# Gate logits from the values' normalised tokens instead of a second normalisation

## The chip, the cores and the metric

One core of one Trainium2 chip runs the kernel. The metric is the device time of one execution in microseconds; a lower time is better.

## The reference

The input is `x` of shape (4, 56, 56, 128): four images of 3136 tokens with 128 channels. Four layers follow one another: a neighbourhood attention with a feed-forward part, a recurrence over a spectrum, a softmax attention with a mixture of eight experts (two per token), and the layer that this change touches. The last layer is, for the tokens `t` of one image:

```
t = t + L3_attn(ln(t))        # q, k, v from ln(t); attention = softmax(exp(-|q-k|^2)) @ v
x = ln(t)                     # normalised over the 128 channels, no weight, no bias
logits = x @ gate_w.T + gate_b                  # 64 experts
probs  = softmax(logits, over the tokens)
vals, idx = top_k(probs of each expert, 8)      # eight tokens for every expert of every image
pooled = sum over the 8 of vals * x[idx]        # one vector per expert and image
out    = second product of a gelu feed-forward of the expert on pooled
result = t + scatter_add(out * vals at idx)
```

In the attention of this layer, `exp(-|q-k|^2)` is practically zero for every pair of tokens, so the softmax is uniform and the attention adds one and the same vector `v = Wv mean(ln(t))` to all tokens of an image. The kernel uses that, and verifies on the chip with bounds on the distances that it holds.

## The kernel before

**Sizes.** An image's tokens lie in `NT` = 28 tiles of `P` = 112 tokens; `GT` = 4 tiles make a group, so an image has `NG` = 7 groups of `GW` = 448 tokens. A tensor with tokens on the partitions is 112 x 512 per group; turned, it is 128 x 448. There are `EC` = 64 experts and `KT` = 8 tokens for each.

**Two layernorms.** For the last layer the kernel normalises each token twice: once before the mean of the values is known (`g_st`, `g_rs`, `g_off` in `span_norms`, `xn` in `normal`, line L1693) and once after `v` has been added (`c_st`, `c_rs`, `c_off` in the choice's `statistics` and `root`, `xn` again by `normal`). `FarAttention.of` makes the first: four `xn` per group on ACT, four transposes on PE (`turned`, L208 is the helper that records every transpose), a copy `xnT` that also sums over the tokens (L1813), the products q and k with bfloat16 casts (`products`) and their norms (`with_norms`). `FarAttention.mean` makes `v` from the sums (`x_total`, `v_ps` L1883, `v` L1887) and `add` adds it to the tokens (`x` L1892 on DVE). `bounds` are the bfloat16 products `d_ps` (L1861), each followed by an ACT relu with a sum (L1873) or a DVE reduction (L1867); one piece of it is called a half.

**The expert choice** is `ExpertChoice.steps`. For each group: `statistics` (four DVE instructions, L2301), then `root` (a Newton iteration on DVE, `inverse_root`, L909 ff.), `store` (two DMAs on SP: the tokens, then `c_rs` as a column of single numbers, into the DRAM table `rows` that the later gather reads), and then by group `tokens` (`normal`: four ACT instructions, for image 3 every second on POOL, L1688), `turned` (four PE transposes, one ACT copy `zT` L2322), and `logits` (PE product `l_ps` L2327, ACT copy `taken` L2331, DVE MAX8 `best` L2332, which takes from the PSUM). After all groups, `choose` finds the positions of the eight largest (FIND_INDEX8, L2351) and POOL gathers the rows (L2355), `marked` marks them (L2363), `weighed` multiplies (L2377), and `pooled` reduces.

**Where the work lies.** `Attention.run` is layer 2's softmax attention, one image after another, made of score products `s_ps` (L2066) and output products `o_ps` (L2149). Between these, `Paced` calls pieces of a background list as their due times come. A piece has a cost, which fixes its due time in its list, and can be marked `apart`, so that no second of its list begins in the same step. Behind image 2's attention stand the mixtures and far pieces of images 0 and 1 and the choice of image 0 (`chosen(0)`, merged with the bounds); behind image 3's stand the mixture and far pieces of image 2 and the choices of images 1 and 2. `trail(3)` lets the groups of image 3 follow its own attention block by block (places "t").

The order that results is written out and rearranged by a scheduler for each engine; each engine then runs its queue in order. After the attention, a part with an order written out by hand follows (`tc.manual_schedule`, L3006): the last group's far pieces, `mean`, `add` and `statistics`, `root` for groups 0 to 2 and for groups 3 to 6, then `tokens`, `turned` and `logits` of the seven groups of image 3 interleaved by hand with halves (`beside`), the choice, and after it `experts`, which streams 32 weight lots of 1 MB, and `scatter`. Nine lots are requested before the mean.

Of the kernel before, what the change touches and what calls it, by code (L numbers as in the profile page):

```python
# [1699 lines left out]
class FarAttention:  # L1700
# [16 lines left out]
    def __init__(self, env, ctx, flow, work):  # L1717
        self.env, self.flow, self.work = env, flow, work
# [31 lines left out]
    def weights(self):  # L1750
# [25 lines left out]
        def of_values():  # L1776
            ps = flow.one([128, 512], "w_ps")
            nc.tensor.transpose(ps[:, :C], loaded("w_v", ins["L3_attn_Wv"]), env.ident)
            self.v_w = cp.tile([128, C], F32, tag="v_w", name="v_w")
            nc.vector.tensor_copy(self.v_w, ps[:, :C])  # L1780
# [13 lines left out]
    def image(self, b, spans, places="d"):  # L1794
# [4 lines left out]
        x = env.x[b]  # L1799
        held = {"q": {}}  # L1800
        pool = self.held[1 - b % 2]

# [75 lines left out]
        def mean():  # L1878
            total = sp.tile([128, 1], F32, tag="x_total", name="x_total")
            nc.vector.tensor_reduce(total, held["sums"], AX.X, ALU.add)  # L1880
            nc.vector.tensor_scalar(total, total, 1.0 / TOK, None, ALU.mult)
            v_ps = flow.one([128, 512], "v_ps")
            nc.tensor.matmul(  # L1883
                v_ps[:P, :C], total.to_broadcast([128, P]), self.v_w, start=True, stop=True
            )
            held["v"] = v = sp.tile([P, C], F32, tag="v", name="v", bufs=1)
            nc.vector.tensor_copy(v, v_ps[:P, :C])  # L1887

# [8 lines left out]
        def of(span):  # L1897
            take, norm = span_norms(env, sp, b, span, places)

            def tokens(g):  # L1900
                held["xn"] = normal(
                    env, self.work, places, b, g, norm, span, places == "t" and g == NG - 1
                )

            return [costing(1.8 * len(span), take)] + sum([
                [
                    costing(0.6, lambda g=g: tokens(g)), costing(0.6, lambda g=g: turned(g), True),
                    costing(0.8, lambda g=g: products(g), True),
# [308 lines left out]

class ExpertChoice:
# [9 lines left out]
    def __init__(self, env, ctx, flow):  # L2228
# [24 lines left out]
        ]  # L2253
        self.fold = cp.tile([2 * EC, EC], F32, tag="fold", name="fold")
        nc.gpsimd.tensor_tensor(self.fold, env.ident[:, :EC], env.ident[:, EC:], ALU.add)
        self.lots, self.at = {}, 0

# [7 lines left out]
    def pieces(self, b, places="d"):  # L2265
# [5 lines left out]
        for g in range(NG):  # L2271
# [10 lines left out]
    def steps(self, b, places, norms_of):  # L2282
# [20 lines left out]
        def root(groups):  # L2303
            of = slice(groups[0] * GT, (groups[-1] + 1) * GT)
            mean2, var = moments(env, sp, f"c{len(groups)}", st[:, of, :])
            inverse_root(env, sp, var, rs[:, of])
# [26 lines left out]

        def store(groups):
            of = slice(groups[0] * GT, (groups[-1] + 1) * GT)
            rows_of = self.rows[b].rearrange("(t p) c -> p t c", p=P)
# [54 lines left out]
        def pooled():  # L2391
# [13 lines left out]
            logits=logits, choose=choose, marked=marked, weighed=weighed, gather=gather,  # L2405
# [100 lines left out]
    def scatter(self):  # L2506

        env, nc, flow = self.env, self.env.nc, self.flow
        for pair in range(2):
# [4 lines left out]
            bias = self.late.tile([2 * EC, C], F32, tag="c_bias", name="c_bias")  # L2514
# [382 lines left out]
def layers_of_safe_scores(env: Env, f, soft):  # L2897
    with ExitStack() as ctx:
# [63 lines left out]
        def chosen(b):  # L2962
            return listed("far", held["choice"].pieces(b))

        def to_mixture():
# [3 lines left out]
            held["far"] = far = FarAttention(env, right, flow, held["choice"].work)  # L2969
# [36 lines left out]
        with tc.manual_schedule(  # L3006
# [5 lines left out]
            *tail, products, with_norms = held["tails"][-1]  # L3012
# [17 lines left out]
            for g in early:  # L3030
                add[g]()
                of["statistics"](g)
                beside("scalar", 1)
            of["root"](early)
            of["store"](early)
            each("statistics", late)
            beside("scalar", 1)
            of["tokens"](0), of["tokens"](1), of["turned"](0), of["logits"](0)
            of["root"](late)
            of["store"](late)  # L3040
            of["turned"](1), of["tokens"](2), of["logits"](1), of["turned"](2), of["logits"](2)
            beside("scalar", 1)
            of["tokens"](3), of["tokens"](4), of["turned"](3)
            of["tokens"](5), of["logits"](3), of["turned"](4)
            of["tokens"](6), of["logits"](4), of["turned"](5), of["logits"](5)
            of["turned"](6), of["logits"](6)
# [90 lines left out]
```

## Time and profile before

| | |
|---|---|
| median of 3 runs | 2461.78 us |
| lowest and highest | 2459.37 and 2465.88 us |
| the profiled execution | 2462.98 us, of which its span is 2461.2 us |
| granted TensorE clock, mean of the span | 0.965 |
| busy share of PE, DVE, ACT, POOL | 95%, 74%, 63%, 12% |
| last layer-2 attention to the first expert product | 2275 to 2342 us |
| expert products and scatter to the end | 2342 to 2461 us |
| DMA in the last slices of the span | up to 297 GB/s |

Times inside the span are counted from its start. The engines are named PE (matmul), PEld (weight load), DVE, ACT, POOL and SP (the queue that issues most DMAs). A row of groups names the line, the engine, the operation, the output and input, their shapes, the count, then the busy time in us, the mean duration in ns, and the idle time just before with what ended it.

### The profile page before, as it was taken

To read this page: it belongs to the slowest core of one execution; us is meant where nothing else is said; L and a number is where in the kernel's file an instruction comes from. 1 tells how busy PE (TensorE), PEld (TensorE's weight loads), DVE (VectorE), ACT (ScalarE), POOL (GpSimd) and SP (SyncE) were. 2 spreads that over 40 slices of the span, in tenths; PEclk is the share of its full clock that TensorE was granted. 3 is DMA by queue.
4 is the path that set the end of the run, shared out by engine and by line. 5 is a ranking of instruction groups with operands and counts; after the bars stand their busy time and mean duration, and the time that the engine had idled before them with its cause. 6 is when DMAs were issued, how large, how long until landed. Compare 5 with 4: busy or idle time off the path is not lost.

```text
span 2461.2 us, 38767 instructions
## 1 busy us (share of the span) xinstructions
PE 2337.9 (95%) x14357; PEld 1258.2 (51%) x14357; DVE 1816.2 (74%) x4816; ACT 1550.7 (63%) x3346; POOL 293.8 (12%) x578
## 2 busy tenths in 40 slices
PE   6999999999999999999999999999999998998585
PEld 4777777775455555555554444445444443433134
DVE  5666899983997958799678777854788576776554
ACT  4999889875666646676332556575545566775553
POOL 4423363320000000000000000100000001011302
PEclk9999999999999999999999999999999997998578
DMA  5100000000000000000000010000000010100676
GB/s 124 36 8 2 2 2 2 2 2 9 1 1 1 1 1 0 1 1 1 12 1 0 1 27 1 5 1 1 1 1 1 1 27 5 27 5 1 184 297 206
DMA packets 65642, 61.42 MB, mean 25 GB/s; under 512 B 17048, under 2 KB 60915, under 8 KB 61348
## 3 DMA queue, kind: packets, MB, share of 16 engines
q1 hardware_dynamic: 64932, 57.80, 8.4%
q8 instruction: 115, 1.88, 0.3%
q0 software_dynamic: 512, 1.06, 0.2%
q14 instruction: 83, 0.68, 0.1%
HBM read 45.83 MB, written 12.90 MB: 24 GB/s over the span
## 4 chain that ended last, share of the span: by engine, by line
PE 63%; DVE 6%; ACT 2%; DMA 2%; issue 2%; POOL 1%; SPq 0%; DVEq 0%; POOLq 0%; ACTq 0%
PE s_ps L2066 20%; PE o_ps L2149 20%; PE y_ps L1574 7%; PE d_ps L1861 3%; PE xT_ps L208 2%; PE g_ps L1207 2%; DMA lot<-in_L_ffn_lots 2%; PE l_ps L2327 1%; PE y_ps L2090 1%; PE z_ps L2042 1%; PE q_ps L1825 1%; DVE found L1867 1%; PE l_ps L1534 1%; ACT xn L1693 1%; DVE gated L1587 1%
## 5 line engine op out<-in xcount | busy, mean ns | idle before, releaser
L2073 ACT ACTIVATE e<-s_ps 128x448 f32<-128x448 f32 x688 | 366.5, 541 | 491.8 <-PE s_ps L2066 486.1
L2066 PE MATMUL s_ps<-zT,xnT 128*128 128x448 f32 (+1 forms) x1400 | 649.4, 554 | 0.0
L2149 PE MATMUL o_ps<-e,keep 128*128 128x448 f32 (+1 forms) x1376 | 648.5, 554 | 0.0
L2149 PEld LDWEIGHTS o_ps<-e,keep 128*128 128x128 f32 (+1 forms) x1376 | 241.7, 190 | 217.8 <-issue 217.2
L2066 PEld LDWEIGHTS s_ps<-zT,xnT 128*128 128x128 f32 (+1 forms) x1400 | 241.1, 189 | 213.9 <-issue 193.5
L1873 ACT ACTIVATE d_ps<-d_ps,half 128x448 f32<-128x448 f32 (+1 forms) x376 | 227.2, 605 | 88.0 <-PE d_ps L1861 86.3
L1867 DVE TENSOR_REDUCE found<-d_ps 128x1 f32<-128x448 f32 x324 | 196.9, 619 | 77.6 <-PE d_ps L1861 75.7
L1574 PE MATMUL y_ps<-experts,xnT 128*112 128x512 f32 x448 | 217.0, 608 | 0.0
L1587 DVE TENSOR_TENSOR gated<-y_ps,gate 112x512 f32<-112x512 f32 x220 | 148.8, 686 | 35.5 <-PE y_ps L1574 33.0
L1593 DVE TENSOR_TENSOR gated<-gated 112x512 f32<-112x512 f32 x330 | 151.8, 467 | 3.5
L1861 PE MATMUL d_ps<-q_near,k_near 32*128 32x448 bf16 (+1 forms) x700 | 135.4, 374 | 15.6 <-ACT d_ps L1873 10.0
L208 PE MATMUL xT_ps<-ident,xn 112*128 112x112 f32 x672 | 117.8, 283 | 34.1 <-ACT xn L1693 26.0
L208 PEld LDWEIGHTS xT_ps<-ident,xn 112*128 112x128 f32 x672 | 80.4, 147 | 113.5 <-ACT xn L1693 58.9
L1673 POOL TENSOR_TENSOR g_rs<-var,exponent 112x4 f32<-112x4 f32 x17 | 17.9, 1053 | 1006.3 <-DVE var L1672 895.3
L1574 PEld LDWEIGHTS y_ps<-experts,xnT 128*112 128x112 f32 x448 | 77.2, 180 | 98.9 <-issue 63.8
L1861 PEld LDWEIGHTS <-k_near 32*128 32x128 bf16 (+1 forms) x700 | 32.0, 92 | 181.2 <-issue 167.2
L1693 ACT ACTIVATE xn<-x,g_off,g_rs 112x128 f32<-112x128 f32 x220 | 93.2, 486 | 26.3 <-DVE g_off L1675 13.0
L677 DVE TENSOR_TENSOR e<-e,band 112x1792 f32<-112x1792 f32 (+3 forms) x56 | 99.9, 1788 | 10.2 <-ACT e L670 10.2
L782 PE MATMUL f_ps<-w_fc,h 128*112 128x128 f32 x896 | 104.8, 274 | 1.9 <-ACT h L773 1.6
L782 PEld LDWEIGHTS f_ps<-w_fc,h 128*112 128x112 f32 x896 | 99.8, 177 | 5.2 <-ACT h L773 4.8
L768 PE MATMUL h_ps<-zT,w_fc 128*128 128x448 f32 x224 | 88.9, 540 | 0.6 <-ACT zT L762 0.6
L670 ACT ACTIVATE e<-s_ps 112x1792 f32<-112x1792 f32 (+3 forms) x56 | 82.6, 1476 | 6.3 <-PE s_ps L661 3.3
(427 smaller groups left out, 3939.7 us busy)
## 6 DMA issues: line engine op xcount, KB each, us to landing
lot<-in_L_ffn_lots SPq DMA_DIRECT2D x32, 1024.0 KB
out_x<-x SPq DMA_DIRECT2D x28, 224.0 KB
x<-in_x SPq DMA_DIRECT2D x3, 1568.0 KB
rows<-x SPq DMA_DIRECT2D x3, 1568.0 KB
x<-in_x SPq DMA_DIRECT2D x7, 224.0 KB
parts<-in_waves SPq DMA_DIRECT2D x8, 173.0 KB
out<-found SPq DMA_DIRECT2D x60, 2.0 KB
rows<-x SPq DMA_DIRECT2D x1, 896.0 KB
```

The lines of the kernel that those rows point to most:

```text
L208: self.nc.tensor.transpose(ps[:, j * P : (j + 1) * P], xn[:, j, :], self.ident[:P, :P])
L782: nc.tensor.matmul(f_ps[:, j, :], h[:, k, j * P : (j + 1) * P], w_fc2[:, k, :], start=(k == 0), stop=(k == 3),)
L1574: nc.tensor.matmul(y_ps, held["xnT"][g][:, j * P : (j + 1) * P], self.experts[:, 4 * i : 4 * i + 4, :], start=True, stop=True,)
L1587: nc.vector.tensor_tensor(gated[:, some, :], y_ps, gate[:, some].unsqueeze(2).to_broadcast([P, 4, C]), ALU.mult,)
L1593: by.tensor_tensor(gated[:, :n, :], gated[:, :n, :], gated[:, n : 2 * n, :], ALU.add)
L1693: env.nc.scalar.activation(xn[:, j, :], env.x[b][:, g * GT + j, :], AF.Identity, bias=norm["off"][:, i : i + 1], scale=norm["rs"][:, i : i ...
L1861: nc.tensor.matmul(d, held["k"][part, 128 * c : 128 * c + n], held["q"][g][part, :], start=True, stop=True,)
L1867: nc.vector.tensor_reduce(self.found[:, self.most : self.most + 1], d, AX.X, ALU.max)
L1873: nc.scalar.activation(d, d, AF.Relu, bias=self.half[:n], accum_out=self.found[:n, self.sums : self.sums + 1],)
L2066: nc.tensor.matmul(s_ps[i * n : (i + 1) * n, :GW], self.xnT[:, at : at + n], zT, start=True, stop=True,)
L2073: nc.scalar.activation(e[:n], s_ps[:n, :GW], AF.Exp)
L2149: nc.tensor.matmul(sums[:, :GW], self.keep[:n, k, :], e[:n], start=(k == 0 and g - 1 not in pairs), stop=last,)
```

## The change

The second layernorm and its turn are not done any more. With `d = 1/g_rs`, `w` the gate weights with their mean over the channels taken off, and `m = w v` (one number per expert), the logits of a token are

```
logits = c_rs * (d * (w xn) + m)
```

where `xn` is the token normalised before `v` was added. `w xn` is made in the far pieces from `xnT`, right after it was turned for q and k. The product of Wv with `w` is made once in the setup and `m` from it with one small matmul per image.

The per-token scales `d` and `c_rs` lie with tokens on the partitions, but the logits have experts on the partitions and tokens in the row. For images 0 to 2, `keep_scales` stores both into DRAM and `fetch_scale` fetches them group by group, broadcast over 64 partitions; POOL multiplies by `d`, and DVE adds `m` and multiplies by `c_rs` in one instruction, then takes the maximum from the SBUF (`moved`). For image 3, `d` of the first six groups is fetched and multiplied in the far pieces; `d` of the last group and all of `c_rs` are spread with PE products of a broadcast column and the identity (`spread`), and the DVE instruction reads the result from the PSUM. `root` for image 3 uses a POOL power in place of the Newton iteration. The part written out by hand is shorter: seven `moved`, each followed by one half.

```
 FarAttention.weights / of_values
+            self.choice.centre()
-            nc.vector.tensor_copy(self.v_w, ps[:, :C])
+            nc.tensor.matmul(
+                ps[:, C : C + EC], w_v, self.choice.gate_w, start=True, stop=True
+            )
+            nc.vector.tensor_copy(self.v_w, ps[:, : C + EC])
 FarAttention.image / mean
+            m_ps = flow.one([128, 512], "m_ps")
+            nc.tensor.matmul(m_ps[rows, :1], self.v_w[:, C:], total, start=True, stop=True)
+            nc.scalar.copy(choice.moved[b // 2][rows], m_ps[rows, :1])
 FarAttention.image / of
+            def deviations():
+                held["sd"] = sd = sp.tile([P, n], F32, tag=f"g_sd{n}_{places}", name="g_sd", bufs=1)
+                nc.vector.reciprocal(sd, norm["rs"])
+                if not final:
+                    choice.keep_scales(b, 0, span, sd)
+                    return
+                ps = flow.one([128, 512], "sd_ps")
+                choice.spread(ps, rows, sd)
+                held["row"] = row = sp.tile([128, GW], F32, tag="row_t", name="row", bufs=1)
+                nc.scalar.copy(row[rows], ps[rows, :GW])
             def tokens(g):
...
+                if trailing and not final:
+                    held["row"] = row = sp.tile([128, GW], F32, tag="row_t", name="row", bufs=1)
+                    choice.fetch_scale(row[rows], b, 0, g)
+            def logits(g):
+                cols = slice(g * GW, (g + 1) * GW)
+                l_ps = flow.one([128, 512], "l_ps")[rows, :GW]
+                nc.tensor.matmul(l_ps, choice.gate_w, held["xnT"], start=True, stop=True)
+                if final:
+                    nc.vector.tensor_tensor(raw[:, cols], l_ps, held["row"][rows], ALU.mult)
+                    return
+                nc.scalar.copy(raw[:, cols], l_ps)
+                if trailing:
+                    nc.gpsimd.tensor_tensor(
+                        by_tile(raw[:, cols]), by_tile(raw[:, cols]),
+                        by_partition(held["row"][rows]), ALU.mult,
+                    )
 ExpertChoice
+    def keep_scales(self, b, i, span, scale):
+        of = slice(span[0], span[-1] + 1)
+        self.env.nc.sync.dma_start(
+            self.scales[b][i].rearrange("g (p j) -> p g j", p=P)[:, of],
+            scale.rearrange("p (g j) -> p g j", j=GT),
+        )
+    def fetch_scale(self, row, b, i, g):
+        self.env.nc.sync.dma_start(row, self.scales[b][i][g].partition_broadcast(EC))
+    def spread(self, ps, rows, scale):
+        for j in range(GT):
+            self.env.nc.tensor.matmul(
+                ps[rows, j * P : (j + 1) * P], scale[:, j : j + 1].to_broadcast([P, EC]),
+                self.env.ident[:P, :P], start=True, stop=True,
+            )
 ExpertChoice.pieces, for images 0 to 2 (from_raw=True): in place of tokens, turned, logits
+            for cost, name in ((0.1, "fetched"), (1.4, "moved")):
+                first.append(costing(cost, lambda name=name, g=g: steps[name](g)))
 ExpertChoice.steps
         def root(groups):
-            inverse_root(env, sp, var, rs[:, of])
+            if last:
+                nc.vector.tensor_scalar(var, var, 1e-5, None, ALU.add)
+                nc.gpsimd.tensor_tensor(
+                    rs[:, of], var, env.exponent[:P, : var.shape[1]], ALU.pow
+                )
+            else:
+                inverse_root(env, sp, var, rs[:, of])
+        def fetched(g):
+            held["scale"] = scale = [
+                self.work.tile([128, n], F32, tag=f"{tag}_d", name="scale", bufs=1)[rows, :GW]
+                for tag, n in (("xn", GT * C), ("xnT", GW))
+            ]
+            for i in range(2):
+                self.fetch_scale(scale[i], b, i, g)
+        def moved(g):
+            part = taken[:, cols]
+            if last:
+                ps = flow.one([128, 512], "rs_ps")
+                self.spread(ps, rows, rs[:, g * GT : (g + 1) * GT])
+                scale = ps[rows, :GW]
+                nc.vector.scalar_tensor_tensor(
+                    part, part, self.moved[b // 2][rows], scale, ALU.add, ALU.mult
+                )
+            else:
+                apart, scale = held["scale"]
+                nc.gpsimd.tensor_tensor(
+                    by_tile(part), by_tile(part), by_partition(apart), ALU.mult
+                )
+                nc.vector.scalar_tensor_tensor(
+                    by_tile(part), by_tile(part), self.moved[b // 2][rows],
+                    by_partition(scale), ALU.add, ALU.mult,
+                )
+            nc.vector.max(held["best"][rows, g * KT : (g + 1) * KT], part)
         def store(groups):
+            if not last:
+                self.keep_scales(b, 1, groups, rs[:, of])
 the part written out by hand, image 3
+            logits()
             of["root"](early)
             of["store"](early)
             each("statistics", late)
-            beside("scalar", 1)
-            of["tokens"](0), of["tokens"](1), of["turned"](0), of["logits"](0)
+            beside("scalar", 2)
             of["root"](late)
             of["store"](late)
-            of["turned"](1), of["tokens"](2), of["logits"](1), of["turned"](2), of["logits"](2)
-            beside("scalar", 1)
-            of["tokens"](3), of["tokens"](4), of["turned"](3)
-            of["tokens"](5), of["logits"](3), of["turned"](4)
-            of["tokens"](6), of["logits"](4), of["turned"](5), of["logits"](5)
-            of["turned"](6), of["logits"](6)
+            for g in range(NG):
+                of["moved"](g)
+                beside("scalar", 1)
             of["choose"]()
```

## The prediction

> **What bounds the kernel now.** The page came first, its engine line and its slices. Digits are tenths of a slice of 61.5 us; PEclk is the granted TensorE clock.
>
> ```profile
> PE 2337.9 (95%) x14357; PEld 1258.2 (51%) x14357; DVE 1816.2 (74%) x4816; ACT 1550.7 (63%) x3346; POOL 293.8 (12%) x578
> ...
> PE   6999999999999999999999999999999998998585
> ...
> PEclk9999999999999999999999999999999997998578
> DMA  5100000000000000000000010000000010100676
> ```
>
> TensorE is busy at 9 tenths from slice 1 on (counted from 0) except in slice 33, where busy share and clock dip, and in the last slices; only there is room. In the attention phase (1380 to 2275 us) only what leaves or enters PE's queue moves the end; work taken off ACT, DVE or POOL there is worth nothing by itself.
>
> Next, the table by windows. Columns: stretch, length, busy us (instructions) of PE, weight load, DVE, ACT, POOL, granted clock, DMA share, GB/s.
>
> ```profile
> 2020.00:2040.00 20.00, 19.66 (x79) 8.21 (x77) 7.87 (x18) 17.14 (x45) 0.00 (x0) 1.00 0.08 1
> 2040.00:2060.00 20.00, 15.62 (x47) 6.31 (x47) 9.98 (x33) 13.66 (x35) 1.01 (x1) 0.65 0.00 1
> 2060.00:2080.00 20.00, 18.55 (x42) 6.23 (x41) 13.90 (x27) 13.19 (x28) 6.21 (x10) 0.75 0.06 14
> 2280.00:2300.00 20.00, 8.52 (x24) 3.09 (x24) 13.45 (x56) 9.55 (x27) 10.85 (x13) 0.50 1.00 408
> 2300.00:2320.00 20.00, 14.57 (x33) 5.08 (x34) 6.03 (x22) 10.72 (x25) 3.49 (x8) 0.50 0.92 146
> 2320.00:2340.00 20.00, 9.71 (x30) 1.85 (x28) 14.58 (x25) 12.34 (x29) 5.09 (x11) 0.50 0.06 13
> ```
>
> Two places fall short: 2040 to 2080 (image 1's choice, clock 0.65 and 0.75) and the tail (image 3's choice, PE half idle at clock 0.50). The waits of PE name the first, and PE's groups from 2045.5 to 2065.6 show what it cost:
>
> ```profile
> PE xT_ps L208 <- ACT xn L1693: 2.7, 1, 2.7
> ```
> ```profile
> L2327 PE MATMUL l_ps<-zT,gate_w 128*64 128x448 f32 x6 | 4.9, 911 | 1.0 <-ACT zT L2322 1.0
> L208 PE MATMUL xT_ps<-ident,xn 112*128 112x112 f32 x12 | 4.3, 428 | 2.7 <-ACT xn L1693 2.7
> ```
>
> In that stretch the list had put choice transposes, gate matmuls and bound products one after another with no attention matmul between; PE waited 2.7 us for ACT's normalised tokens, and the clock's events show 0.5 from 2046.0 to 2069.9. A transpose took 428 ns, not 259, a gate matmul's instruction 911, not 564.
>
> Last, the chain of waits through the tail (start, length, what):
>
> ```profile
> 2294.74 1.65 ACT xn L1693 x4
> 2296.39 0.49 ACT zT L2322
> 2296.88 0.04 issue
> 2296.93 1.75 PE l_ps L2327 x2
> 2298.68 0.95 PE xT_ps L208 x4
> 2299.65 0.54 ACT zT L2322
> ...
> 2321.27 0.54 ACT taken L2331
> 2321.83 0.65 DVE best L2332
> ```
>
> Seven groups go through one loop, copy 0.54, gate product 1.75, transposes 0.95: 3.3 us each, 2294.7 to 2322.5. From there the pick runs serially to the first expert product at 2342.
>
> **The sum** is made against the profiled execution, 2462.98 us (span 2461.2 and 1.78 around it), 1.20 above the median of 2461.78.
>
> *A. PE work in the attention phase.* Images 0 to 2 lose 21 groups of four transposes. At full clock four take 0.47 us of PE time (pitch of 228 instructions from 1384 to 2040: 26.8 us). Two lie wholly in the slow stretch, so 19 x 0.5 = -9.5. Their 21 gate matmuls only move into the far pieces, each with its ACT copy (0.526). Image 3's first six groups bring theirs from the tail: 6 x 0.9 (pitch per matmul, two instructions) = +5.4. Centring the gate and the extra product with Wv: +1. A = -3. ACT loses 84 normalisations (0.488) and 21 copies (0.531) here, DVE gains 21 fused products (0.615, the row of L2377): off PE's path, counted at nothing. PE's own queue covers them; without that cover DVE's is +13.
>
> *B. The slow stretch.* From the gate product at 2045.5 to the next attention product at 2065.6 there are 20.0 us holding 7.8 us of work at full pitch; with the half-speed tail to 2069.9 it lost about 14.5. In the changed order of PE's queue no run without attention matmuls is estimated over 5 us (the longest before: 14.7), and the chain xn, transposes, copy, gate product is gone. I take -12; bounds 0 (a like stretch forms elsewhere) and -17.
>
> *C. Setup and copies of the mean* (four m_ps products beside v_ps, 0.335 each by that row, ACT copies): inside A's rounding.
>
> *D. The tail.* Added ahead: the last group's reciprocal on DVE, four PE spread matmuls and an ACT row copy stand in front of its normalisation: 0.2 + 1.75 (as one gate product at half clock) + 0.5 = +2.4. The second Newton root (12 steps of about 0.2) becomes one POOL power (1.05, row L1673), as does the first: about -1.2 each. Then seven `moved` steps with no round trip between them: on DVE one fused product from PSUM (0.68, row L1849) and one MAX8 (0.65), 1.35 each, 9.5 in all; on PE four 112-column matmuls that together stream as many columns as one gate product (1.75 at half clock) and a bound half (about 0.5): 2.3 each, 16 in all. The early statistics ended at 2290.35; with 2.4, a root of 1.9 (0.5 of small steps, the power, 0.35), four late groups' statistics (0.88 each) and the second root of 1.9 the first `moved` starts near 2300, and the last maximum falls between 2310 and 2317 by which engine limits; I take 2313.5 against 2322.5: D = -9, bounds -12 and -5. The rows' store, landed by 2316.6, still ends before the gather needs it; a last maximum before 2312 would make it late next.
>
> *E. New waits.* Before each choice `c_rs` is stored (SP, behind nothing, but ahead of 1.6 MB of rows), then each group fetches two broadcast rows on SP; POOL multiplies, DVE fuses. Nearest rows: a 64 KB load landed in 1.5 us, the 12.5 KB of 4-byte elements (`rows<-c_rs`) in 4.9 alone; so root to first fetch is some 6 us, against 4 to 7 us of other DVE work queued between: up to 2 us of DVE wait per image, and up to 1 us per group where the list leaves under 2 us between `moved` steps. SP gets 58 DMAs more in all (10 stores, 48 fetches of 64x448); its own queue holds little else then: the lots of 1 MB are issued only after the last far piece, so nothing waits behind these but the rows' stores and, for the trailing groups of image 3, one fetch and one POOL product each. Both scale buffers are single, so a fetch waits for the step before. One fetch of image 1 stands on SP behind a 10.6 us rows store; POOL's multiply waits for it, and behind POOL's queue the next power `g_rs`, which ACT's normalisation and PE's transposes need. POOL gains 27 products of about 1.1 us (L2539's 1274 ns x 448/512). The floor is 0, attention work hiding all (a gain is excluded: nothing here is removed); the ceiling is 21 x 1 = 21. PE has other matmuls queued through most of it, so I take near the floor, +4.
>
> The port shared by DVE and POOL speaks against E's floor: in the tail a DVE step on 12 columns (L938) took 1.12 us beside a POOL add, 0.17 elsewhere. The Trainium skill, SBUF — State Buffer, "SBUF: two separate sides", says that a DVE instruction with two SBUF inputs and a GpSimd instruction reading SBUF lock each other out for the whole instruction; by it alone every one of the 27 products could block one DVE step, which DVE's 26% of idle time absorbs or not as E's bounds say.
>
> A + B + D + E = -3 - 12 - 9 + 4 = -20: 2443 profiled, **2442** on the median's scale.
>
> On the clock the row says that 2.7 us of idle was enough for 24 us at half speed. The Trainium skill, TensorE: Matmul & The Clock Gate, "HAM oscillation", blames idle gaps over about 3.4 us; by it a fetch wait of 2 us costs its own length alone, by the row several times that.
>
> **Rivals.**
>
> *The slow stretch stays (15%).* Far pieces still hold xn, transposes and copies in series, and one PE wait of over 2 us is enough. Then B = 0: 2454. Against it: the changed queue spreads them between attention matmuls.
>
> *Slower: fetches stall POOL and through `g_rs` PE (17%).* Place: the seven `moved` steps of images 0 to 2. Price: if a PE idle of over 2.5 us follows in each image, three stretches like the present one, 3 x 14.5 = 43, replace E's 4: 2482; with two, 2467. Decides where the fetch lands over 3 us after the DVE's queue reaches `moved`. For it: single buffers, in-order SP, 4.9 us small-element stores. Against: PE's queue holds attention work throughout, and only the mixture pieces behind `g_rs` would run late.
>
> *The tail is bound by PE at half clock (inside my forecast).* 16 us from 2301: last maximum 2317, D = -5, time 2446.
>
> *It doesn't do what it says (3%).* The unscaled logits need their own normalisation only if transposes remain; the queue shows 112 fewer, so little speaks for it.
>
> **How the numbers follow.** My forecast 65%, spread 2432 to 2450 by the terms' bounds. The low end of the range is A at its best (0.6 per four transposes, 0.75 per gate product: -7) with B -17, D -12 and E +2: -34, so 2428 on the median's scale; 2427 taken. The high end takes in the stretch that stays and part of the slow rival, 2466. A tenth lies above, less below. What a measurement of this kernel can tell from no change is about 0.3%, 7.4 us: faster means under 2454.4, slower over 2469.2. Forecast and two fifths of the first rival are faster: 0.65 + 0.06 = 0.71; the rest of that rival (0.09), the part of the slow rival in which two images stall (0.03) and the change without effect (0.03) are the same: 0.15; the slow rival's rest, 0.14, is slower.
>
> **What would show it.** Right: L208 down by 112 transposes, no window of 20 us between 1400 and 2270 under clock 0.9, first fetch landing before DVE is ready, last MAX8 of the tail about 33 us after the last `g_rs` (2280.33 before) rather than 42. Wrong: PE waits on POOL or DVE `moved`, DVE idle released by DMA of the scales, half-clock stretches about 1520, 2050 or 2150, or a tail loop over 2.5 us per group.

## The result, and the profile after

The change made the kernel slower: 2484.4 us median (2482.4 to 2486.1) beside 2461.5 us of the kernel before, a ratio of 1.0090 with an interval of 1.0073 to 1.0108. The profiled execution took 2483.9 us, its span 2482.1. The forecast was 2442. The experiments ran on several chips, on which the median of the kernel before was 2458.1 to 2461.7 us; so from here on every ratio is against the kernel before on the same chip, and differences in us between versions are worked out from their ratios.

The page of the changed kernel, engine line and slices (62.1 us each):

```profile
PE 2335.6 (94%) x14321; PEld 1255.3 (51%) x14321; DVE 1842.6 (74%) x4827; ACT 1511.2 (61%) x3238; POOL 327.9 (13%) x593
...
PE   6999999999999999999999999999999999998575
...
PEclk9999999999999999999999999999999999998588
DMA  5100000000000000000000011000000011200576
```

At this grain almost nothing is seen: ACT lost 40 us of work, POOL gained 34, the dip of the clock in slice 33 is no longer a digit. The windows show it (columns as before):

```profile
2020.00:2040.00 20.00, 14.79 (x44) 5.31 (x43) 12.56 (x37) 8.20 (x21) 6.43 (x5) 0.95 0.51 97
2040.00:2060.00 20.00, 17.61 (x65) 7.11 (x65) 16.73 (x57) 13.83 (x36) 8.21 (x7) 0.88 0.16 37
2060.00:2080.00 20.00, 12.73 (x39) 5.87 (x37) 9.37 (x19) 7.04 (x19) 5.34 (x6) 0.74 0.27 41
2300.00:2320.00 20.00, 8.59 (x28) 3.52 (x28) 8.75 (x32) 8.66 (x26) 11.99 (x12) 0.52 0.85 341
2320.00:2340.00 20.00, 14.49 (x61) 9.24 (x62) 11.95 (x35) 7.88 (x23) 3.38 (x2) 0.50 0.85 214
```

From 2020 to 2080 PE works 45.1 of 60 us (before: 53.8 in the same stretch), and ACT and DVE have no more to do than PE. So the engines stand still together, and not for lack of queued work. The waits of PE (2030 to 2080) and of DVE (2000 to 2080) name what they wait for:

```profile
PE xT_ps L208 <- ACT xn L1693: 13.3, 2, 7.3
```
```profile
DVE g_off L1675 <- POOL g_rs L1673: 8.7, 2, 7.5
DVE taken L2451 <- DMA scale<-scale: 4.0, 1, 4.0
```

The timelines of SP, POOL, DVE, ACT and PE give the first of the two stalls link by link (start, length, engine and line, and in brackets the idle time before with what ended it):

```profile
2026.03 0.58 SPq L2462 DMA_DIRECT2D rows<-x  x1
2029.83 9.61 SPq L2333 DMA_DIRECT2D scale<-scale  x2
```
```profile
2037.62 1.35 POOL L2448 TENSOR_TENSOR taken<-taken,scale 64x448 f32<-64x448 f32 x1 [7.81 <-DMA scale<-scale]
2039.05 1.01 POOL L1673 TENSOR_TENSOR g_rs<-var,exponent 112x4 f32<-112x4 f32 x1
```
```profile
2031.89 0.14 DVE L1672 TENSOR_SCALAR var<-var 112x4 f32<-112x4 f32 x1
2031.95 0.61 DVE L1875 TENSOR_REDUCE found<-d_ps 128x1 f32<-128x448 f32 x1
2040.09 0.16 DVE L1675 SCALAR_TENSOR_TENSOR g_off<-sums,g_rs 112x4 f32<-112x4 f32 x1 [7.53 <-POOL g_rs L1673]
```
```profile
2040.29 1.65 ACT L1693 ACTIVATE xn<-x,g_off,g_rs 112x128 f32<-112x128 f32 x4 [7.17 <-DVE g_off L1675]
```
```profile
2040.83 0.83 PE L208 MATMUL xT_ps<-ident,xn 112*128 112x112 f32 x2 [6.04 <-ACT xn L1693]
```

In order of time: SP issues the store of 1.6 MB of rows, then the fetch of a scale, which lands 7.8 us later instead of the usual 2.67. POOL's product with 1/g_rs waits for that. The variance of image 3's next group is ready on DVE at 2032.0, but its power stands behind the product in POOL's queue and starts at 2039.05. DVE's next instruction, `g_off`, needs the power, so DVE stands still for 7.5 us with everything behind it, then ACT for 7.2, then PE for 6.0. The late fetch of one row of scales stops four engines.

The second stall (7.3 us of PE idle up to 2073.3) is the same with DVE in POOL's place: its fused product waits 4.0 us for a row of `c_rs` that was only just stored, and the variance that POOL's power needs stands behind it. The chain of waits shows it, and POOL's timeline two products that ran beside it:

```profile
2060.63 6.26 DMA scale<-scale
2066.91 1.84 DVE taken L2451
...
2069.83 0.18 DVE var L1672
2070.14 1.02 POOL g_rs L1673
2071.18 1.31 DVE g_off L1675
```
```profile
2066.60 1.34 POOL L2448 TENSOR_TENSOR taken<-taken,scale 64x448 f32<-64x448 f32 x1 [6.58 <-DMA scale<-scale]
2071.12 1.34 POOL L2448 TENSOR_TENSOR taken<-taken,scale 64x448 f32<-64x448 f32 x1
```

Two DVE instructions are longer here than elsewhere, the fused product (1.84 us, median 1.02) and `g_off` (1.31 us, 0.16 in the first stall), both beside a POOL product; together that is some 2 of the 7.3 us.

In the tail the chain of waits of the changed kernel shows one step of the seven, and their end:

```profile
2330.24 1.72 PE rs_ps L2338 x8
2331.97 0.50 PE d_ps L1869
2332.47 0.02 issue
2332.49 0.73 ACT d_ps L1881 x2
...
2342.34 0.64 DVE best L2455
```

The last steps take 3.06 us each and are serial: spread 1.72 to 1.77, bound products 0.5, ACT's sum 0.73. From the start of the last `g_rs` to the last maximum it is now 39.5 us (2303.5 to 2343.0), before 42.2.

The loss of this profile, 20.9 us of span, lies in the attention phase (the last output product of layer 2 starts at 2265.1, before at 2246.6: +18.5) and between that and the last `g_rs` (+4.6: the transposes, the gate, q, k and norm products of the group before the last all come behind the last output product now; before, its transposes came ahead); the tail gives 2.7 back. The kernel's description and the prediction count the attention phase to 2275 us; that takes in the mixture of the last group.

### The profile page after: what moved, and what is told of

Read it like the earlier page. It is cut to its first block, busy times and chain, and to the rows that moved or that the text cites. A ratio compares the mean times of both kernels' runs of the same rounds, so it can differ in the third digit from the quotient of the medians.

```text
span 2482.1 us, 38731 instructions
## 1 busy us (share of the span) xinstructions
PE 2335.6 (94%) x14321; PEld 1255.3 (51%) x14321; DVE 1842.6 (74%) x4827; ACT 1511.2 (61%) x3238; POOL 327.9 (13%) x593
## 4 chain that ended last, share of the span: by engine, by line
PE 58%; DVE 9%; DMA 4%; ACT 2%; POOL 2%; issue 1%; SPq 0%; DVEq 0%; POOLq 0%; ACTq 0%
PE s_ps L2106 18%; PE o_ps L2189 18%; PE y_ps L1574 7%; PE d_ps L1869 3%; PE g_ps L1207 2%; PE xT_ps L208 2%; DMA scale<-scale 2%; DMA lot<-in_L_ffn_lots 2%; DVE found L1875 1%; PE l_ps L1933 1%; PE q_ps L1833 1%; DVE gated L1587 1%; PE y_ps L2130 1%; PE z_ps L2082 1%; PE l_ps L1534 1%
## 5 line engine op out<-in xcount | busy, mean ns | idle before, releaser
L1869 PE MATMUL d_ps<-q_near,k_near 32*128 32x448 bf16 (+1 forms) x700 | 137.3, 376 | 21.6 <-ACT d_ps L1881 10.2
L1673 POOL TENSOR_TENSOR g_rs<-var,exponent 112x4 f32<-112x4 f32 x17 | 18.1, 1062 | 894.6 <-DVE var L1672 894.5
L208 PE MATMUL xT_ps<-ident,xn 112*128 112x112 f32 x560 | 94.2, 277 | 27.3 <-ACT xn L1693 18.9
L208 PEld LDWEIGHTS xT_ps<-ident,xn 112*128 112x128 f32 x560 | 64.8, 144 | 82.9 <-ACT xn L1693 43.4
```

Of the source, the lines that this page charges most:

```text
L208: self.nc.tensor.transpose(ps[:, j * P : (j + 1) * P], xn[:, j, :], self.ident[:P, :P])
L1869: nc.tensor.matmul(d, held["k"][part, 128 * c : 128 * c + n], held["q"][g][part, :], start=True, stop=True,)
```

## The experiments

A table of the attention phase, worked out from PE's records from 1200 us to the last output product: gaps and durations are summed, and the time at half clock is from the clock's events. Each row is the one profiled execution, in us.

| kernel | last output product | PE idle | PE busy | at half clock |
|---|---|---|---|---|
| before | 2246.6 | 12.4 | 1033.5 | 30.2 |
| the change | 2265.1 | 32.9 | 1032.0 | 34.1 |
| scales resident, 8 byte step | 2232.7 | 7.6 | 1024.9 | 10.2 |
| scales resident, 16 byte step | 2241.2 | 11.2 | 1029.4 | 13.3 |
| product with 1/g_rs early | 2248.9 | 19.3 | 1029.6 | 23.9 |
| the same, c_rs resident | 2235.9 | 11.5 | 1024.2 | 6.8 |

The last column is not wholly due to waits: in the change, 6.8 of its 34.1 us (from 1788.7) follow a stretch in which no gap of PE is over 0.05 us.

**Which images.** First, images 0 to 2 as before (`from_raw=False`, no `deviations` and no `logits` in their far pieces, no `keep_scales`), image 3 as changed:

```
-            return listed("far", held["choice"].pieces(b, from_raw=True))
+            return listed("far", held["choice"].pieces(b))
...
-                    costing(0.6, lambda g=g: logits(g), True),
+                    *([costing(0.6, lambda g=g: logits(g), True)] if trailing else []),
```

> Only image 3 takes its logits from the values' tokens; images 0 to 2 normalise and turn a second time as before. Theory (the fetches of the scales in images 0 to 2 cost the time, the tail gains the 2.6 us that the two profiles show): the attention phase goes back to its old length plus six gate products (about 5 us), so 2459 to 2467 us. Rival (the loss lies in image 3's steps, or in the reordered queue as a whole): 2475 us or more.

Measured: ratio 1.0048 (1.0032 to 1.0063), 2469.1 us. The theory gave at most 2467 and the rival at least 2475, so this is between the two. In the profile PE's time to the last output product grew by some 11 us of work and 2.8 of idle; six gate products are 5.4 of that by the prediction's price, and time at half clock rose to 37.5 us; the tail gave back 2.7. So image 3's part alone is a loss as well. That its gate products moved out of the tail, where PE has room, into the attention phase, where it has none, explains about half of the 11 us; the rest is not followed further.

Then the reverse, images 0 to 2 as changed, image 3's far pieces, `root` and hand-written order as before:

```
-            trailing, n = places == "t", len(span) * GT
+            trailing, n = False, len(span) * GT
...
-            for g in range(NG):
-                of["moved"](g)
-                beside("scalar", 1)
+            of["tokens"](0), of["tokens"](1), of["turned"](0), of["logits"](0)
+            ...
```

> Images 0 to 2 as in the change, image 3 as before. Theory: the loss stays, less the six gate products that stay in the tail, plus the 2.6 us of the tail: 2477 to 2488 us. Rival (image 3's steps): within 6 us of 2461 us.

Measured: 1.0095 (1.0071 to 1.0119), 2479.7 us, PE idle 31.3. The first three images' part alone loses as much as the whole change. The two parts do not add up (0.48% and 0.95% against 0.90% together); that each moves the other's pieces is the likely reason, not a shown one.

**Waits or work.** Both scales read from a resident tensor of other numbers, the instructions left as they are:

```
-            for i in range(2):
-                self.fetch_scale(scale[i], b, i, g)
+            held["scale"] = [
+                self.bias1.rearrange("q c e -> q (c e)")[rows, : 2 * P]
+                .rearrange("q (p j) -> q j p", p=P)[:, :1, :].to_broadcast([EC, GT, P])
+            ] * 2
...
```

> In images 0 to 2 both scales are read from a resident tensor of other numbers, so no fetch is made and the selection differs; all engine instructions stay (the resident rows are read with a step of 8 bytes, the fetched ones of 16). Theory (waits for the fetches): most of the loss goes, 2445 to 2462 us. Rival (load and port contention of POOL's 21 products and DVE's 21 fused products, or the order of the queues): 2475 us or more.

Measured: 0.9917 (0.9898 to 0.9936), 2438.6 us: by the ratios some 43 us less than the change, and, at 2441 us on the scale of the first chip, where the forecast was. The same windows of this kernel:

```profile
2020.00:2040.00 20.00, 19.71 (x71) 7.35 (x70) 16.98 (x57) 15.49 (x41) 2.35 (x2) 1.00 0.24 35
2040.00:2060.00 20.00, 18.86 (x69) 8.75 (x67) 18.45 (x54) 11.39 (x30) 2.46 (x4) 1.00 0.13 2
2060.00:2080.00 20.00, 19.82 (x57) 6.84 (x56) 18.73 (x47) 14.21 (x32) 5.88 (x10) 1.00 0.06 14
```

PE is full at full clock. All 21 POOL products and 21 fused DVE products are still made, so neither their number nor their place beside one another is the main cost. (The fetched rows also lay in buffers that the far pieces use; in the trace of the change no engine but SP waits for these to come free.) But this kernel changed two things: the resident row has a step of 8 bytes between its numbers, the fetched rows one of 16. So it was run again with 16 (`p=P // 2`, and the same with eight parts of 56):

> As the kernel with resident scales, but these are read with the step of 16 bytes that the fetched rows have, so that the fused DVE instruction and the POOL product last as long as in the change (1.07 and 1.42 us in place of 0.67 and 1.18); no fetch, other numbers. Theory (waits): within 4 us of the kernel with the 8 byte step. Rival (length of the strided instructions carries part of the gain): 2448 us or more.

Measured: 0.9953 (0.9936 to 0.9970), 2450.3 us, which is the rival's number and not within the theory's 4 us; the two intervals touch only at 0.9936. The rows of the fused DVE product, in this order of the kernel with an 8 byte step, with 16, and (from the version with the first groups on PE, below) read from the PSUM without a step:

```profile
L2449 DVE SCALAR_TENSOR_TENSOR taken<-taken,moved,bias 64x448 f32<-64x448 f32 x21 | 14.1, 674 | 0.2
```
```profile
L2448 DVE SCALAR_TENSOR_TENSOR taken<-taken,moved,bias 64x448 f32<-64x448 f32 x21 | 21.3, 1018 | 0.2
```
```profile
L2448 DVE SCALAR_TENSOR_TENSOR taken<-taken,moved,rs_ps 64x448 f32<-64x448 f32 x9 | 6.0, 672 | 2.1 <-PE rs_ps L2337 2.0
```

So of the 43 us some 34 (1.0090 to 0.9953) are the waits for the fetches and some 9 (0.9953 to 0.9917) the longer strided instructions, each to about 6 us by the intervals. By their rows the strided instructions are 7 us of DVE and 4 of POOL. DVE's work is not free in these stretches.

**Which wait.** The product moved from POOL to DVE:

```
-                nc.gpsimd.tensor_tensor(
+                nc.vector.tensor_tensor(
                     by_tile(part), by_tile(part), by_partition(apart), ALU.mult
```

> In images 0 to 2 the product with 1/g_rs is made on DVE in place of POOL; the fetches stay. If POOL's queue is what delays g_rs (the 7.5 us wait of DVE on it near 2030 us), that wait goes but DVE takes over the waiting for the fetch: gain of 0 to 10 us against the change, 2474 to 2485 us. If the port shared by POOL and DVE were the cost, DVE steps beside it fall to their usual length and the gain is larger, 2465 us. If DVE's load is the cost: 2490 us or more.

Measured: 1.0085 (1.0063 to 1.0106), 2477.4 us: not separable from the change. PE idle fell to 26.0, and one stall of 6.5 us at 2059 remained where there were two. DVE now does 0.96 us per group more (20 us in all) and its own wait for `c_rs` is still there (11.9 us). The gain that the shared port would have given, to 2465 us, did not come; the added DVE work could hide part of it, so the kernel with resident scales, which keeps the POOL products, is the stronger sign that this port is not the main cost.

The product made in the far pieces of every image, right after the gate product, as for image 3; the choice fetches `c_rs` alone:

```
-                if trailing and not final:
+                if not final:
                     held["row"] = row = ...
...
-                apart, scale = held["scale"]
-                nc.gpsimd.tensor_tensor(
...
+                scale = held["scale"]
```

> As the change, but the product with 1/g_rs is made in the far pieces of every image, with its row fetched when the group is normalised; the choice of images 0 to 2 fetches only c_rs and has no POOL product. Theory (POOL's queue waits for fetches and g_rs stands behind): POOL's waits go, DVE's for c_rs stay: 2450 to 2468 us. Rival (load of POOL and port contention): the same 21 products remain, so no gain, 2475 us or more.

Measured: 1.0031 (1.0014 to 1.0047), 2465.1 us. The same work, 0.6% less time: the wait for 1/g_rs cost about 14.5 us (1.0090 to 1.0031, to about 6 us), and one of the two stalls is gone. The other is left, and this version shows it alone. SP's and DVE's timelines, image 1:

```profile
2043.32 0.30 SPq L2325 DMA_DIRECT2D scale<-c_rs  x1
2043.66 0.54 SPq L2457 DMA_DIRECT2D rows<-c_rs  x1
2046.03 30.56 SPq L2332 DMA_DIRECT2D scale<-scale  x7
```
```profile
2051.89 1.01 DVE L2445 SCALAR_TENSOR_TENSOR taken<-taken,moved,scale 64x448 f32<-64x448 f32 x1 [3.86 <-DMA scale<-scale]
```

The store takes 2.7 us until SP can issue the fetch, and the fetch 5.8 us behind the rows' single numbers, together 8.6 us from the store's issue to the first scaling; DVE had 4.7 us of other work and then stood still for 3.9. With `c_rs` resident instead (16 byte step):

> As the version with the product with 1/g_rs in the far pieces (its rows are fetched there), but c_rs is read from a resident tensor of other numbers with a 16 byte step. Theory (what that version still loses is DVE's wait for c_rs behind its store): 2436 to 2446 us, some 22 us less than with the fetch of c_rs. Rival (the fetches in the far pieces cost it): 2455 us or more.

Measured: 0.9938 (0.9917 to 0.9960), 2446.0 us, at the upper edge of what the theory gave. The wait for `c_rs` is worth some 23 us (1.0031 to 0.9938), more than its 11.5 us of DVE idle (four waits). Between the two profiles the last output product comes 13.0 us earlier (8 us of PE idle go, and time at half clock falls from 23.9 to 6.8 us), and the stretch from there to the last `g_rs` falls from 37.4 to 29.8 us, since the transposes, gate, q and k products of the group before the last come ahead of the last output product again.

**Two edits that left the time as it was.** A second pair of buffers, used alternately, and the rows' store placed after the last `moved` (the first also leaves out `c_off`, an instruction of `root` that the change no longer needs, and shares three small tiles to make room; so do the versions with all waits taken away, below):

```
+                for tag, n in (own if g % 2 else (("xn", GT * C), ("xnT", GW)))
```
```
+            first.append(costing(0.05, lambda: steps["keep"](range(NG))))
...
+        first.append(costing(0.1, lambda: steps["store"](range(NG))))
```

> As the change, but the fetched scales of images 0 to 2 lie alternately in the old pair of buffers and in a second pair of their own, so that SP can fetch the next group's while this one's are used (three small tiles are shared to make room). Theory (a cycle of fetch 2.67 us, POOL product 1.36 us, next fetch, held by single buffers): the cycle shrinks to under 3 us and POOL and DVE wait less: 2455 to 2470 us. Rival (only the first fetch, behind the store of c_rs and of the 1.6 MB of rows, matters): 2475 us or more.

> As the change, but in images 0 to 2 the rows of 1.6 MB are stored after the last group's scaling, so that no fetch stands behind them on SP. Theory (round trip of every fetch): gain of one wait of about 7 us per image at most, and of one late g_rs: 2470 to 2482 us. Rival (the rows' store alone makes the fetches late): 2445 to 2460 us.

Measured: 1.0092 (1.0075 to 1.0108) and 1.0094 (1.0078 to 1.0111). In the first, POOL's products still follow each other at 4.2 us (2017.1, 2021.3, 2025.5), since SP still waited for the transfer and the product before; but the seven fetches of `c_rs` of image 0 came in 18.1 us in place of 28.4, and nothing was gained. So the cycle of later fetches is not what costs; that was the rival. In the second, SP's timeline has the rows' store at 2023.8 ahead of a fetch at 2027.7 as before: the scheduler moved it ahead. The second tells neither for nor against the theory.

**All waits at once.** The product early, `c_rs` fetched two groups ahead into two own buffers, 4 us of space in the list, and image 3's spread in the score banks (the PSUM tiles in which layer 2's attention had its score products):

```
+                [128, GW], F32, tag=f"scale{g % 2}", name="scale", bufs=1
...
+            first.append(costing(4.0, lambda: None))
...
-                ps = flow.one([128, 512], "rs_ps")
+                ps = flow.scores()
```

> All waits taken away at once with all work kept: the product with 1/g_rs in the far pieces, c_rs fetched two groups ahead into two buffers of its own, a space of 4 us of other pieces between its store and the first scaling, the rows stored last; and in the tail the spread rows lie in the score banks, so that PE needs not wait for ACT's bound sums. Theory: the time of the kernel without fetches, less up to 5 us of the tail, plus a little: 2432 to 2445 us, faster than the kernel before. Rival (the long strided DVE and POOL instructions cost it): 2455 us or more.

Measured: 0.9984 (0.9969 to 0.9998), 2454.2 us, 2447.6 to 2466.5. Better than both kernels by a little, and just short of the rival's 2455. DVE still waited 2.7, 3.8 and 2.9 us for the first fetch. The profiled execution, 2464.9 us, is the second longest of twelve, with 51.2 us at half clock before the last output product. With 14 in place of 4:

> As the version with all waits taken away at once, but 14 us in place of 4 us of other pieces are put between the first fetch of c_rs and the first scaling of images 0 to 2, where DVE still waited 2.7, 3.8 and 2.9 us. Theory (DVE's wait for the round trip of c_rs is what is left): 2436 to 2448 us. Rival (order of the queues or long strided DVE instructions): 2452 us or more.

Measured: 0.9982 (0.9969 to 0.9995), 2455.4 us, within the rival's range. But the edit made no space: DVE's waits for the fetch were 16.8 us in three, up to 8.4, because the scheduler set the scaling right behind the root all the same (8.4 to 9.8 us from the last step of the root to the first scaling, as without the space). So it left open what was still lost. So the first three groups got `c_rs` by PE's spread, as image 3 has it, and only groups 3 to 6 fetch:

```
-            if last:
+            if last or g < 3:
-                ps = flow.scores()
+                ps = flow.scores() if last else flow.one([128, 512], "rs_ps")
```

> As the version with all waits taken away at once, where DVE still waited up to 8.4 us for the first fetch of c_rs, since the queue's order moved the scaling ahead of the space; here groups 0 to 2 of images 0 to 2 get c_rs by PE's spread into the PSUM (nine groups at 0.75 us: +7 us of PE) and only groups 3 to 6 fetch it, so no instruction has to wait for a store and a fetch. Theory (that first wait is what is left of the loss): 2440 to 2450 us. Rival (length and number of the added instructions): 2453 us or more.

Measured: 0.9950 (0.9933 to 0.9966), 2450.9 us beside 2461.7, the fastest of the versions that leave nothing out, and faster than both kernels: no wait of DVE or POOL for a fetched scale is left in its attention phase, PE idle 9.9 us in place of 19.4 in the version before. So that first wait was a part of what was left. It was not all: the intervals don't separate this version from the one with `c_rs` resident (0.9938), but in the profiles its last output product comes 16 us later (2252.1 against 2235.9), about 7 of them the nine spreads, with 27.3 us at half clock against 6.8, and its tail (30.3 us against 39.5) gives 9 back. What makes the rest of the 16 is open.

The last one stores 1/g_rs in the row's order, so that POOL reads without a step:

```
+        order = "g (p j) -> p g j" if i else "g (j p) -> p g j"
```

> As the version with the first three groups on PE, but 1/g_rs is stored in the order of the row (4 byte elements), so that POOL's product reads its row without a step. Theory (a strided read makes the 27 POOL products 0.25 us longer and DVE steps beside them wait): 1 to 4 us less than with the step. Rival (the product lies beside other work): the same within 2 us.

Measured: 0.9965 (0.9952 to 0.9978): not faster. POOL's product fell from 1.379 to 1.154 us, but POOL waited 107 us for the rows in place of none, with one wait of DVE for a scale (3.8 us) back. The rows are now stored in four times as many elements; that this makes them late is likely and not shown by a run of its own.

**The tail.** Only image 3's spread in the score banks, everything else as changed:

> As the change, but the spread rows of image 3 lie in the two score banks and not in the ring of four that the bound halves use. Theory (each of the seven tail steps is one serial round of PE spread 1.75 us, bound products 0.5 us and ACT sums 0.73 us, because the ring holds one step and a third): the step falls from 3.06 us to about 2.3 us and the time by about 5 us, 2474 to 2481 us. Rival (PE alone sets the step, or DVE): no change.

Measured: 1.0080 (1.0059 to 1.0101), 2481.9 us, which the intervals don't separate from the change. The tail of its profile does: from `g_rs` to the last maximum 37.1 us instead of 39.5. PE's waits from 2300 to 2352, of the change and then of this version:

```profile
PE rs_ps L2338 <- ACT d_ps L1881: 3.3, 4, 0.9
```
```profile
PE s_ps L2338 <- DVE taken L2443: 3.8, 1, 3.8
```

The ring of PSUM buffers was one link; freed from it, PE waits once for DVE. DVE is late there because of `c_off`: the change still computes it and nothing reads it, and DVE, with sixteen statistics queued behind the first one, stood still 2.4 and 3.0 us for POOL's two powers before it. Without `c_off` but with the ring (the second pair of buffers) the stretch took 38.1 us, without both (the version with all waits taken away) 33.2.

## Why the prediction was wrong

**The failing step is E.** It named the right chain, fetch on SP behind the rows' store, POOL's product, `g_rs` behind it, and the wait for `c_rs` after its store; and it priced it at +4 with a ceiling of 21. The runs give about +43: 34 of waits by the resident pair (14.5 for 1/g_rs and 23 for `c_rs` by the other two versions, the same within their intervals) and 9 of strided reads. Four things were wrong in its size:

- *"PE has other matmuls queued through most of it."* It had, for 2 us: in the first stall DVE stops at 2032.6 and PE at 2034.8. DVE and POOL run their queues in order, so a late row of 64x448 stops reductions, statistics and `g_off` that have nothing to do with it, and with them ACT and PE. The reserve that counts is the work queued ahead of the waiting instruction on its own engine, and then the reserve of each engine behind it.
- *The late `g_rs`.* It was named, with no price of its own beside the up to 1 us per group. The fetch behind 1.6 MB of rows took 7.8 us, and 6.0 of them reached PE.
- *The round trip of `c_rs`.* Estimated at 6 us from a 64 KB load and a 12.5 KB store; measured 8.6. The fetch took 2.67 us alone and over 5 behind the single numbers that are stored in between.
- *The instructions.* The fused product took 1.02 to 1.07 us, not the 0.615 of a row with the same shape: that row's second operand is bfloat16 and read without a step. POOL's product was put at 1.1 and took 1.35. And DVE's 26% idle share, an average over the kernel, did not hide it.

One count of E was off without weight: SP got 12 stores of scales, not 10; the 48 fetches were right.

**A** was right in its direction. In the trace of the change the transposes from 1200 us to the last group but one fell from 360 to 276 and by 11.4 us (start to start), and the gate products rose by 12 instructions and 3.3 us: -8 against the -3 of the sum. It shows only when the waits are gone (PE busy 1024.2 instead of 1033.5).

**B** failed with E. The stretch of 23.9 us at half clock is gone, but new ones, 27.3 us of them at the four waits for scales, make 34.1 us at half clock instead of 30.2. With the scales resident it is 10.2: most of the forecast -12 was there to be had, under a condition that the change itself broke.

**D** had the right sign and a third of the size: 2.7 us instead of 9. The bound of PE at half clock (2.3 us a step) was taken as the slow case; the real step was serial over PE and ACT, 3.06, since its three PSUM tiles come from a ring of four. And the two powers, put at 1.05 each by a row of 4 columns, took 2.28 and 2.90 us on 12 and 16 columns, with DVE waiting for both. With the ring and `c_off` out of the way the stretch is 33.2 us, the 33 of the forecast. And image 3's part was not paid for at all by this: alone it cost 0.48%.

**The rival** that came true is the slow one, at 17%: its place and its mechanism are those of the trace. Its price assumed three stretches at half clock like the one before; the profile has two stalls of 6 and 7 us, with little more time at half clock than before. So its 2482 lies near the measured 2484 by luck. The point from which it decides, 3 us late, was passed: DVE waited 3.7 us in image 0 and 4.0 at 2063, POOL 7.8.

The prediction read from the profile of before that 2.7 us of idle was enough for 24 us at half speed. The order of time does not bear that out. The clock's events have half speed from 2045.95, and PE's idle came after it, from 2046.9 to 2049.6:

```profile
2045.52 1.36 PE L2327 MATMUL l_ps<-zT,gate_w 128*64 128x448 f32 x2 [0.42 <-ACT zT L2322]
2049.55 0.45 PE L208 MATMUL xT_ps<-ident,xn 112*128 112x112 f32 x1 [2.67 <-ACT xn L1693]
```

In the 8 us before 2045.95 no gap is over 0.61 us, so what set that stretch off is open. The Trainium skill (TensorE: Matmul & The Clock Gate, "HAM oscillation") names idle gaps of over about 3.4 us. In the changed kernel an idle of 2.7 us that ended at 1507.9 was followed by 3.4 us at half clock, and half clock began within one of 2.8 us that ended at 2175.4 and lasted 6.8; and the 6.8 us from 1788.7 had no idle before them at all. So neither the page's figure nor the prediction's reading accounts for every stretch of this case.

The rule of the shared port (SBUF — State Buffer, "SBUF: two separate sides") fits the rows: DVE's `x<-x,v` took 803 ns on the mean of images 0 to 2 against 683 before, with two of 1.65 and 1.80 us in image 0 while POOL's products stood in the same stretch, and 685 where these were made earlier. 21 of these steps at 0.12 us are 2.5 us of DVE, and the two long instructions of the second stall some 2 more; it is not the main cost.

## What to carry to other kernels

A DMA that an instruction waits for is priced by what stands behind that instruction on its own in-order queue, not by the bytes: ask for each queue what is next, and follow it to PE. Work that only needs early data (here 1/g_rs) belongs where its data is made; data that is only just stored should not be fetched back at once where it can be spread on chip. A due time or a later place in the program changes nothing until the order of the queues shows that it did: look there before the time.

## What was not expected of the hardware

- A fused DVE product of 64x448 float32 took 0.67 us with an operand read at a step of 8 bytes (or without a step from the PSUM) and 1.02 us at 16 bytes; POOL's product 1.18 and 1.38 us, 1.15 without a step. The Trainium skill, GPSIMD Engine Reference, "Performance pitfalls for Q7 kernels", has a cliff above a step of 8 bytes for that engine's own programs, half more per element; here, from 8 to 16 bytes, it is 18% for POOL's product and 51% for DVE's.
- 112 KB that are broadcast to 64 partitions from a row of 1.8 KB landed in 2.67 us on a quiet queue, 7.8 behind a store of 1.6 MB, and over 5 behind 3136 single numbers.
- Twelve runs of the version with all waits taken away spread over 0.8% (2447.6 to 2466.5 us), more than the four of the change (0.15%). The granted clock goes with it, 0.974 in the shortest and 0.964 in the longest; why it differs from run to run is open.
